# The last group's edge slots and root rows in a relational graph layer: paced over 61 calls in place of 70

## The chip, the cores and the metric

The kernel runs on one core of a Trainium2 chip. The core has five engines with a queue of instructions each: TensorE (PE in the profile, its weight loads PEld), VectorE (DVE), ScalarE (ACT), GpSimd (POOL) and SyncE (SP). The engines run side by side and wait for one another by semaphores; an engine works off its own queue in order. Transfers between device memory and the on-chip memory are issued from the queues of SP, ACT and POOL and share 16 DMA engines. TensorE writes its sums to PSUM, eight banks of 128 x 512 float32.

The metric is device time in microseconds of one execution, as the median of the runs shown. Line numbers (L356) are those of the kernel before.

## The reference

One layer of a relational graph network with a highway gate, over 1250 nodes of 1024 features, 20000 edges and 8 edge types, all in float32:

```python
h = jnp.maximum(_layernorm(x, axis=-1), 0.0)
...
out = h @ root + bias
for r in range(weight.shape[0]):              # 8 types
    mask = (edge_type == r).astype(h.dtype)
    sums = jax.ops.segment_sum(h[src] * mask[:, None], dst, num_segments=n)
    cnt = jax.ops.segment_sum(mask, dst, num_segments=n)
    out = out + (sums / jnp.maximum(cnt, 1.0)[:, None]) @ weight[r]
u = out
z = jnp.concatenate([u, h], axis=1) @ w_gate + b_gate
x = x + jnp.tanh(u) * z + h * (1.0 - z)
```

## The kernel before

**Matrices and pairs.** The order of sums and products is swapped: the kernel multiplies h by each of the eight weights, writes the products y to device memory, and then adds up, for each node, the rows of y that its edges name. Eleven matrices go through TensorE one after the other (the list `mats`): 0 to 7 the weights, 8 the root, 9 the lower half of w_gate (its product with h is the z of the gate, without u's part), 10 the upper half of w_gate, which multiplies u. The 1250 rows are ten blocks `d` of up to 128; blocks i and i + 5 form pair i, 0 to 4. One pair and one matrix are one call of `product`: seven products of 128 x 512 x 512 (a 2 x 2 scheme with seven in place of eight multiplications; some of the seven are split once more in the same way, by `Second` and `Third`, for pairs 0 to 3). The sums of weight blocks that this scheme needs (t1 to t4, L169 to L181) are made by VectorE during pair 4 of the matrix before (t1 to t3) and pair 0 (t4). A product leaves PSUM by a copy on ScalarE (L380, L395, L402, L406, L429) or an addition on VectorE (L373, L381, L389, L309 to L311) into one of four `row` tiles, and a finished row tile is stored by SP (L475): to y for matrices 0 to 7, to `hr_dram` for the root, to `z_dram` for matrix 9. A row tile is filled anew only once its store has landed.

**Calls.** After each of the seven products `done()` calls `between(j)`, j = 0 to 6. So a matrix has 35 calls, and from the start of matrix 8 to the end of matrix 9 there are 70: call 1 is (matrix 8, pair 0, j = 0), call 70 is (matrix 9, pair 4, j = 6). All other work is written into the program at these calls. The schedule is by hand: the order of the program is the order in each engine's queue.

**Edge slots.** Edge types 0 to 4 are group 0, types 5 to 7 are group 1, the last. For each group the nodes are sorted by how many edges they have, so that block d needs only K[g][d] slots; for group 1 these are 20, 10, 8, 7, 7, 6, 5, 5, 4, 3, in sum 75. A slot (`add_slot`) is one gather on POOL of up to 128 rows of y into a tile `got` (L1165) and one multiply-add on VectorE, u = got * w + u (L1170). There are four `got` tiles (GOT), so a gather waits until the multiply-add four slots earlier is through. For group 1 the tile u starts with the sums of group 0, gathered from `u_dram` (L586).

**The generator `edges`.** It yields once a tick, t = -1, 0, 1 and so on. With LATE = 4 the slots stand at t = 4 to 78, block after block, for the last group in the order 4 to 9, then 0 to 3. GOT = 4 ticks after a block's last slot its `to` is called. For blocks 4 to 9 this stores u to `last_dram` (L1373, on SP). For blocks 0 to 3, which stay on the chip as `us`, it is `add_hr`: a gather of the root's rows from `hr_dram` into a `got` tile (L586), and three ticks later the addition to u (L1380). The generator yields 87 times; the first, without work for the engines, is taken before the pacing starts.

**The pacing.** `spread` hands out ticks over calls: with `total` ticks and `parts` calls, at call n it brings the ticks run to `total * n / parts`, rounded up, and at call `parts` runs whatever is left. For the last group `total` is 75 + 2 + 4 = 81 and `parts` is 70.

**The gate.** Matrix 10 needs u transposed. `gate_u(i, j)` prepares pair i of the gate (blocks 2i and 2i + 1) one pair ahead: at j = 2 it gathers rows of h into two `got` tiles and takes tanh(u) on ScalarE (L1445), at j = 3 it transposes u on TensorE (L322) and makes the left sums (L327, L338), at j = 4 it subtracts the h rows (L1453), which frees the two `got` tiles. For gate pair 0 this happens beside pair 4 of matrix 9, the last pair of that matrix, for gate pair 1 beside pair 0 of matrix 10. `gate_load(i + 2, j)` fetches the u of the pair after next back from `last_dram` (L1460) and its root rows by `add_hr`. `gate_rows` gathers x + h and z for the output.

The part of the main function that the change touches, without what it calls:

```python
        blocks = [*range(HELD, ND), *range(HELD)]
        last = edges(LG, blocks, lambda d, u: (add_hr if d < HELD else to_last)(d, u), LATE)
        next(last)
        between = spread(last, sum(K[LG]) + 2 + LATE, 7 * ((NM - 2 - s) * NP + NP - i))
        while s < NM - 1:
            def beside_h(j):
                between(j)
                if (s, i, j) == (NM - 2, NP - 1, 0):
                    gate_bias(0)
                if (s, i) == (NM - 2, NP - 1):
                    gate_u(0, j)

            step(s, i, beside_h)
            s, i = next(steps, (NM, 0))
```

Of the kernel before, what the change touches and what calls it, by code (L numbers as in the profile page):

```python
# [19 lines left out]
def tile_rgcn_highway(  # L20
# [44 lines left out]
    NP = ND // 2  # L65
# [4 lines left out]
    K = ((28, 14, 13, 12, 11, 10, 9, 8, 7, 6), (20, 10, 8, 7, 7, 6, 5, 5, 4, 3))  # L70
# [9 lines left out]
    GOT = 4  # L80
    UB = 4
    LATE = 4
    IDLE = 12

    A11, A12, A22, S1, S2, S3, S4 = range(7)
    A21 = S3
# [34 lines left out]
    def bank():  # L121
        return psum.tile([P, 512], F32, name="ps", bufs=6)
# [318 lines left out]
    NM = len(mats)  # L441
# [125 lines left out]

    for _ in range(IDLE):
        nc.tensor.matmul(bank()[:, :P], ident, ident, start=True, stop=True)
# [72 lines left out]
    with ExitStack() as early:  # L642
# [20 lines left out]
        class Normed:  # L663
# [13 lines left out]
            def spread(self):  # L677
                n = self.n
                nc.vector.bn_aggr(self.mv[:n], self.st[:n].rearrange("p a b -> p (a b)"))
                nc.scalar.activation(self.sd[:n], self.mv[:n, 1:2], AF.Sqrt, bias=eps[:n])  # L680
# [446 lines left out]
        while going[0]:  # L1127
            s, i = next(steps)
# [11 lines left out]
    with ExitStack() as edges_part:  # L1140
# [47 lines left out]
        def edges(g, blocks, to, late=0):  # L1188

            nb = len(blocks)
            starts = [late + sum(K[g][d] for d in blocks[:b]) for b in range(nb + 1)]
            leaves = [starts[b + 1] - 1 + GOT for b in range(nb)]
            reads = [max(-1, starts[b] - 5, leaves[b - UB] if b >= UB else -1) for b in range(nb)]
            u, then = {}, {}
            for t in range(-1, leaves[-1] + 4):
                for b, d in enumerate(blocks):
                    if starts[b] <= t < starts[b + 1]:  # L1200
                        k = t - starts[b]
                        add_slot(u[d], g, d, k, idx[:, g], w_of[:, g])
                for b, d in enumerate(blocks):
                    if t == leaves[b]:
                        then[t + 3] = to(d, u[d])
                if then.get(t):
                    then[t]()
                for b, d in enumerate(blocks):
                    if t == reads[b]:
                        u[d] = first_u(g, d)  # L1210
                yield
# [8 lines left out]
        def spread(e, total, parts):  # L1220

            said = [0, 0]

            def between(j):
                said[0] += 1
                while said[1] < min(total, -(-total * said[0] // parts)):
                    next(e, None)
                    said[1] += 1
                if said[0] == parts:
                    for _ in e:  # L1230
                        pass

            return between
# [27 lines left out]
        def beside(e, total, s, i, last):  # L1261


            between = spread(e, total, 7 * ((last - s) * NP + NP - i))
            while s <= last:
                step(s, i, between)
                s, i = next(steps, (NM, 0))
            return s, i

        s, i = next(steps)  # L1270
        while s <= EARLY:
            step(s, i)
            s, i = next(steps)
# [17 lines left out]
        while s < R0[1]:  # L1291
            step(s, i, on)
            s, i = next(steps)
# [9 lines left out]
        s, i = beside(first_group, sum(K[0]) + LATE + 1, s, i, R0[2] - 1)  # L1303
# [64 lines left out]
        LG = G - 1  # L1368
# [97 lines left out]
        blocks = [*range(HELD, ND), *range(HELD)]  # L1466
        last = edges(LG, blocks, lambda d, u: (add_hr if d < HELD else to_last)(d, u), LATE)
        next(last)
        between = spread(last, sum(K[LG]) + 2 + LATE, 7 * ((NM - 2 - s) * NP + NP - i))
        while s < NM - 1:  # L1470
            def beside_h(j):
                between(j)
# [6 lines left out]
            s, i = next(steps, (NM, 0))  # L1479

        for i in range(NP):
            t = [rows.tile([P, D], F32, name="row") for _ in range(2)]

            def finish(part, of, c0, more=None):
                d = 2 * i + part
                n = nrows(d)
                at = slice(c0, c0 + of.shape[-1])
                to = t[part][:n, at]
                if more is None:
                    nc.vector.tensor_mul(to, of[:n], place_of("d", i, part)[:n, at])  # L1490
                    nc.vector.tensor_add(to, to, place_of("z", i, part)[:n, at])
                else:
                    nc.vector.tensor_mul(more[:n], of[:n], place_of("d", i, part)[:n, at])
                    nc.vector.tensor_add(to, to, more[:n])
# [38 lines left out]
            if i < NP - 1:  # L1533
                product(h_op[i % 2], fac[NM - 1], t, between=beside_u,
                        last=lambda *of: finish(1, *of))
# [28 lines left out]
```

## Time and profile before

| | |
|---|---|
| median of 3 runs | 1376.04 us (1373.76 to 1376.51) |
| the profiled execution | 1373.07 us, its span 1371.1 us |
| TensorE busy | 1344.4 us, 98% of the span |
| VectorE busy | 944.2 us, 69% |
| ScalarE busy | 370.4 us, 27% |
| GpSimd busy | 587.3 us, 43% |
| mean granted TensorE clock | 0.993 |
| multiply-adds of slots, L1170 | 193, 1282 ns each |
| gathers of slots, L1165 | 193, 1298 ns each on POOL |
| device memory read and written | 212.71 MB and 75.66 MB |

A profile is one execution, taken by the hardware profiler. An engine's line gives its busy time; for TensorE, ends are modelled, so busy is not the same as at its peak. A group of instructions is a line of the kernel with engine, operation and tiles, "out<-in", the number of them, busy time and the mean of one, and then the idle time of the engine just before them and who ended it. In the timeline each row is a start, a duration, the engine, the line and the tiles; in brackets stands the idle time before it and its releaser. SPq, ACTq and POOLq are issues of transfers from those queues. The clock is a share of full speed, as the throttle granted it.

### The profile page before, as it was taken

The page shows a single profiled execution, that of the slowest core. Times are in us where ns is not written, and L with a number is a line of the kernel's source. Part 1 is how long each engine was busy: PE and PEld are TensorE (multiplying, and loading weights), DVE is VectorE, ACT ScalarE, POOL GpSimd, SP SyncE. Part 2 cuts the span into 40 slices and gives each one's busy share as a digit, 9 for nine tenths or more (in the row PEclk, how much of TensorE's full clock was granted, in tenths as well). Part 3 has the DMA queues.
Part 4 walks back from the last instruction along what each step waited for, and adds up shares of the span by engine and source line. Part 5 has one row for each costly group of instructions (what it writes and reads, how often), then busy time and mean ns, then how long its engine had stood idle before and what let it go on. Part 6 is the DMA issues. An engine that isn't in the chain of part 4 may idle for free.

```text
span 1371.1 us, 13215 instructions
## 1 busy us (share of the span) xinstructions
PE 1344.4 (98%) x3954; PEld 686.5 (50%) x3954; DVE 944.2 (69%) x1932; ACT 370.4 (27%) x816; POOL 587.3 (43%) x510
## 2 busy tenths in 40 slices
PE   9999999999999999999999999999999999986997
PEld 5444455455445545554554554555455455543443
DVE  6855967876795743426767776877776796656875
ACT  3335566565731111111111111111112111120210
POOL 0001655654562475002444554455356364435641
PEclk9999999999999999999999999999999999998999
DMA  8755766854954351135549689878678936859971
GB/s 306 275 180 149 92 140 142 213 78 116 194 138 109 71 146 22 61 138 184 191 129 329 218 265 354 271 272 294 209 241 317 360 101 219 308 200 280 328 212 58
DMA packets 106908, 271.15 MB, mean 198 GB/s; under 512 B 22692, under 2 KB 24946, under 8 KB 106704
## 3 DMA queue, kind: packets, MB, share of 16 engines
q1 hardware_dynamic: 46640, 120.01, 29.8%
q0 software_dynamic: 44064, 118.28, 27.4%
q10 hardware_dynamic: 16128, 31.98, 7.4%
q8 instruction: 31, 0.51, 0.2%
q14 instruction: 45, 0.37, 0.1%
HBM read 212.71 MB, written 75.66 MB: 210 GB/s over the span
## 4 chain that ended last, share of the span: by engine, by line
PE 75%; issue 9%; DMA 9%; POOL 4%; DVE 2%; SPq 0%; POOLq 0%; ACT 0%; DVEq 0%; ACTq 0%
PE ps L356 60%; PE ps L214 8%; DMA got<-y,idx 6%; PE ps_n L356 3%; DMA got<-hr_dram,node 2%; PE ps_q L214 2%; POOL got L1165 1%; PE ps_n L214 1%; POOL got L586 1%; DMA w<-in_L_gnn_weight_dram 1%; POOL out_dram L592 1%; PE ps_n L903 1%; PE ps L322 0%; POOL h_op L586 0%; POOL w L586 0%
## 5 line engine op out<-in xcount | busy, mean ns | idle before, releaser
L356 PE MATMUL ps<-w,h_op 128*128 128x512 f32 x2512 | 1110.3, 595 | 13.6 <-DVE row L373 11.3
L356 PEld LDWEIGHTS ps<-w,h_op 128*128 128x128 f32 x2512 | 472.7, 191 | 558.2 <-issue 528.4
L1165 POOL DMA_INDIRECT got<-y,idx x193 | 250.6, 1298 | 357.8 <-DVE u L1170 230.8
L1170 DVE SCALAR_TENSOR_TENSOR u<-got,w_of,u 128x1024 f32<-128x1024 f32 (+1 forms) x193 | 247.0, 1282 | 85.5 <-DMA got<-y,idx 82.6
L982 POOL DMA_INDIRECT table<-row_col,at_i x157 | 176.6, 1125 | 157.7 <-DVE at_i L978 73.9
L381 DVE TENSOR_TENSOR row<-row,part 128x512 f32<-128x512 f32 x55 | 37.9, 689 | 123.8 <-ACT part L380 123.8
L429 ACT COPY row<-ps 128x512 f32<-128x512 f32 x50 | 29.3, 585 | 215.5 <-PE ps L356 215.5
L380 ACT COPY part<-ps 128x512 f32<-128x512 f32 x55 | 32.2, 586 | 179.7 <-PE ps L356 179.7
L395 ACT COPY row<-ps 128x512 f32<-128x512 f32 x55 | 32.2, 585 | 175.4 <-PE ps L356 170.7
L214 PE MATMUL ps<-w,w 128*128 128x256 f32 x288 | 71.3, 380 | 0.0
L406 ACT COPY row<-ps 128x512 f32<-128x512 f32 x55 | 32.2, 586 | 139.3 <-PE ps L356 139.3
L214 PEld LDWEIGHTS ps<-w,w 128*128 128x128 f32 x288 | 54.4, 190 | 18.3 <-issue 12.4
L968 DVE SCALAR_TENSOR_TENSOR junk<-k_bc,key_col,before 128x128 f32<-128x128 int32 x157 | 54.9, 350 | 4.2
L908 DVE TENSOR_TENSOR seen<-seen,ps_n 128x100 f32<-128x100 f32 x157 | 40.3, 256 | 24.6 <-PE ps_n L903 20.4
L402 ACT COPY row<-ps 128x512 f32<-128x512 f32 x43 | 25.2, 586 | 115.7 <-PE ps L356 112.1
L214 PE MATMUL ps<-w,h_op 128*128 128x256 f32 x216 | 56.0, 382 | 0.0
L214 PEld LDWEIGHTS ps<-w,h_op 128*128 128x128 f32 x216 | 40.5, 190 | 25.6 <-issue 22.3
L169 DVE TENSOR_TENSOR w<-w,w 128x2048 f32<-128x2048 f32 (+1 forms) x12 | 25.4, 2116 | 39.3 <-PE ps L356 38.2
L885 ACT ACTIVATE is_lo<-io,less_lo 128x128 bf16<-128x128 f32 x157 | 50.2, 391 | 0.7 <-DMA xh_dram<-xt 0.7
L373 DVE TENSOR_TENSOR row<-row,ps 128x512 f32<-128x512 f32 x30 | 20.5, 684 | 37.5 <-PE ps L356 31.3
L623 POOL DMA_INDIRECT node_dram<-ids,pos_i x20 | 28.5, 1426 | 41.1 <-issue 41.1
L356 PE MATMUL ps_n<-w,h_op 128*128 128x512 f32 x96 | 43.2, 592 | 0.0
(215 smaller groups left out, 1183.1 us busy)
## 6 DMA issues: line engine op xcount, KB each, us to landing
y<-row SPq DMA_DIRECT2D x72, 512.0 KB
w<-in_L_gnn_weight_dram ACTq DMA_DIRECT2D x21, 1024.0 KB
w<-in_L_gnn_weight_dram SPq DMA_DIRECT2D x10, 1024.0 KB
k_bc<-keys_dram SPq DMA_DIRECT2D x39, 256.0 KB
l_bc<-los_dram SPq DMA_DIRECT2D x39, 256.0 KB
w<-in_L_gnn_w_gate_dram ACTq DMA_DIRECT2D x6, 1024.0 KB
h_dram<-h_op SPq DMA_DIRECT2D x9, 512.0 KB
u<-in_L_gnn_bias_dram SPq DMA_DIRECT2D x9, 512.0 KB
```

The costliest lines, as they stand in the source:

```text
L214: nc.tensor.matmul(p, a[:, k, :], b[:, k, :], start=(fresh and k == 0), stop=(k == 1), skip_group_check=True)
L356: nc.tensor.matmul(b[:, at], aop[:, i, k, :], w.of[i][:, k, at], start=(fresh and k == 0), stop=(k == KQ - 1), skip_group_check=True)
L380: nc.scalar.copy(d, b)
L381: nc.vector.tensor_add(c22, c22, d)
L395: nc.scalar.copy(c11, b)
L406: nc.scalar.copy(c12, b)
L885: nc.scalar.activation(is_lo[:, i, :], io, AF.Abs, bias=less_lo[:, c0 + i:c0 + i + 1])
L908: nc.vector.tensor_add(seen[j][:, i, :], was, p[:, i, :])
L968: nc.vector.scalar_tensor_tensor(junk, o["k_bc"][:, i, :], key_col[:, c:c + 1], before, op0=OP.is_equal, op1=OP.mult, accum_out=rank[:, c: ...
L982: ins = nc.gpsimd.indirect_dma_start(out=table[:, :], out_offset=bass.IndirectOffsetOnAxis(ap=at_i[:n, i:i + 1], axis=0), in_=row_col[:n, ...
L1165: nc.gpsimd.indirect_dma_start(out=t[:n], out_offset=None, in_=y[g][:, :], in_offset=bass.IndirectOffsetOnAxis(ap=at[:n, d, k:k + 1], axis=0),
L1170: nc.vector.scalar_tensor_tensor(u[:n], t[:n], w, u[:n], op0=OP.mult, op1=OP.add)
```

## The change

A constant AHEAD = 9 is new. The last group's ticks are handed out over nine calls fewer, 61 in place of 70, and `total` is 4 + 75 + 4 + 4 = 87 in place of 81, which is every tick that the generator has. With that the last tick falls on call 61, (matrix 9, pair 3, j = 4). Since calls go on after the last one that is paced, `spread` tests for `>=` in place of `==`. The pacing of the first group, by the same function, is untouched.

```diff
@@ -81,6 +81,7 @@
     UB = 4
     LATE = 4
     IDLE = 12
+    AHEAD = 9
@@ -1226,7 +1227,7 @@
                 while said[1] < min(total, -(-total * said[0] // parts)):
                     next(e, None)
                     said[1] += 1
-                if said[0] == parts:
+                if said[0] >= parts:
                     for _ in e:
                         pass
@@ -1466,7 +1467,8 @@
         last = edges(LG, blocks, lambda d, u: (add_hr if d < HELD else to_last)(d, u), LATE)
         next(last)
-        between = spread(last, sum(K[LG]) + 2 + LATE, 7 * ((NM - 2 - s) * NP + NP - i))
+        between = spread(last, LATE + sum(K[LG]) + GOT + 4,
+                         7 * ((NM - 2 - s) * NP + NP - i) - AHEAD)
         while s < NM - 1:
             def beside_h(j):
                 between(j)
```

## The prediction

> **What bounds the kernel now.** I read the page first (busy shares and slices), then the stages as a table, then who TensorE waits for, then the timeline of the last 170 us engine by engine.
>
> The page's summary and slices (40 slices of 34.3 us):
>
> ```profile
> span 1371.1 us, 13215 instructions
> PE   9999999999999999999999999999999999986997
> PEclk9999999999999999999999999999999999998999
> ```
>
> TensorE sets the end; it has two soft places, slices 36 and 37 and the last. The same by stage; the columns are PE, weight load, DVE, ACT and POOL busy with counts, granted clock, DMA share, GB/s. The stages are matrix 8, matrix 9 up to its last pair, that pair up to the transposes for pair 2 of matrix 10, and one free pair:
>
> ```profile
> 978.39:1095.58 117.19, 117.19 (x330) 61.98 (x329) 82.37 (x103) 19.14 (x37) 57.47 (x47) 1.00 0.82 288
> 1095.58:1188.73 93.15, 93.15 (x273) 51.34 (x272) 71.47 (x90) 16.19 (x32) 47.91 (x37) 1.00 0.60 197
> 1188.73:1274.72 85.99, 71.06 (x177) 32.32 (x176) 56.38 (x58) 16.97 (x24) 40.38 (x30) 0.92 0.79 258
> 1274.72:1300.50 25.78, 25.78 (x73) 12.30 (x72) 22.52 (x27) 5.45 (x8) 15.64 (x14) 1.00 1.01 322
> ```
>
> TensorE is never idle in matrices 8 and 9 until the last pair; only the third stage loses time and clock. TensorE's waits there:
>
> ```profile
> PE ps L356 <- DVE row L373: 11.3, 2, 8.8
> PE ps L322 <- DVE u L1380: 2.7, 1, 2.7
> PE ps L356 <- DVE h_op L327: 0.9, 1, 0.9
> ```
>
> VectorE in turn stands behind slots. Timeline (start, duration, engine, line, operands, idle before and its releaser):
>
> ```profile
> 1199.40 2.75 POOL L586 DMA_INDIRECT got<-h_dram,node  x1 [3.12 <-DVE u L1170]
> 1208.38 1.28 DVE L1170 SCALAR_TENSOR_TENSOR u<-got,w_of,u 128x1024 f32<-128x1024 f32 x1 [4.20 <-DMA got<-y,idx]
> 1209.94 0.99 POOL L1165 DMA_INDIRECT got<-y,idx  x1 [4.53 <-DVE u L1170]
> 1216.41 1.28 DVE L1170 SCALAR_TENSOR_TENSOR u<-got,w_of,u 128x1024 f32<-128x1024 f32 x1 [6.14 <-DMA got<-y,idx]
> 1217.96 0.99 POOL L1165 DMA_INDIRECT got<-y,idx  x1 [7.03 <-DVE u L1170]
> 1246.60 1.23 DVE L1380 TENSOR_TENSOR u<-u,got 128x1024 f32<-128x1024 f32 x1 [8.51 <-DMA got<-hr_dram,node]
> ```
>
> The two h rows for the gate hold two of the four `got` buffers from 1199 until their subtraction at 1226.79, so the last slots go one at a time: gather, 6.5 us, multiply-add, next gather. That pushes the hr gathers of the first gate pair to 1234, into the z stores and u loads, where one takes 12.3 us (1234.32 to 1246.60).
>
> **The change, part by part.** No instruction is added or dropped; ticks move to earlier calls. Before, 81 ticks go over 70 calls (1.157 each) and call 70 runs the rest; after, 87 ticks (the whole generator) go over 61 (1.426 each). Call 61 is pair 3 of matrix 9, j = 4. The `>=` costs nothing: calls 62 to 70 find the generator empty.
>
> *What it takes away.* Call 63 had reached tick 73, so calls 64 to 70 (the last pair) carried slots of t = 73 to 78, six multiply-adds with their gathers, two hr gathers and two hr adds. All go before that pair. What TensorE gets back: the last pair starts at 1188.73 (40 matmuls from 1185.30, the first product of 3.43 us belonging to pair 3), and its transposes come four products later, at 1202.47. Free pairs follow each other every 25.78 us (transposes at 1274.72, 1300.50, 1326.29). So the transposes for pair 2 would stand at 1202.47 + 2 x 25.78 = 1254.03; they stood at 1274.72. **Gain 20.7 us**: 14.9 us of the waits above, 4.7 us of slow clock (8 matmuls in 5.10 us and the next 48 in 23.92, where 3.60 and 20.7 are normal; granted clock 0.50 in 1251 to 1257), 1.1 us of small gaps. From below: if the 8.8 us wait for L373 and its slow clock stay, 20.7 - 8.8 - 4.7 = 7.2.
>
> *What still has to be ready there.* h rows: POOL is free, gathers about 1185, used about 1208. hr rows of gate pair 0 take the h rows' buffers, about 1210, and are added about 1225; 12.3 us, the worst seen, still fits. The u load follows the z stores on SP at about 1216; the slots' lag of 6.5 us gives 1223. VectorE in such a pair is 22.5 of 25.8 us busy without TensorE waiting (last row of the table). I take 1 us lost, between 0 and 3 (the L1380 wait of 2.7).
>
> *What it moves into matrix 8 and 9.* By the end of matrix 8 (call 35) the old pacing had reached tick 41, 37 slots; the new one tick 50, 46 slots. The nine cost VectorE 9 x 1.28 = 11.5 us. VectorE in matrix 8:
>
> ```profile
> L1170 DVE SCALAR_TENSOR_TENSOR u<-got,w_of,u 128x1024 f32<-128x1024 f32 (+1 forms) x36 | 46.0, 1282 | 21.8 <-DMA got<-y,idx 20.9 <-issue 0.7
> L381 DVE TENSOR_TENSOR row<-row,part 128x512 f32<-128x512 f32 x5 | 3.4, 688 | 9.7 <-ACT part L380 9.7
> ```
>
> Busy 82.4 of 117.2, 20.9 waiting for gathers, 11.8 for TensorE (9.7 at L381, 2.1 at L169). So 11.5 fits only into those 11.8, if gather waits do not grow; and they are fixed by the ring: a gather reaches its multiply-add 5.5 to 11.4 us after issue (1052.84 to 1063.02, say), with four buffers. Slot 1 ran at 994.66, slot 37 at 1098.39: 103.7 us for 36 steps, 2.88 each. Of that VectorE waited 11.7 for TensorE; filled with slots, the pitch is (103.7 - 11.7) / 36 = 2.56. The new pacing asks for 117.2 / 50 = 2.35 (50 ticks in 35 calls). Slot 46 at 2.56 comes at 994.66 + 45 x 2.56 = 1109.9, where 1098.4 is on time: **11.4 us late**.
>
> What waits behind a late slot:
>
> ```profile
> 1070.72 0.68 DVE L309 TENSOR_TENSOR row<-row,ps_n 128x512 f32<-128x512 f32 x1
> 1071.42 2.33 SPq L475 DMA_DIRECT2D hr_dram<-row  x3
> 1078.61 0.59 ACT L402 COPY row<-ps 128x512 f32<-128x512 f32 x1 [2.80 <-PE ps L356]
> 1094.88 2.28 DVE L177 TENSOR_TENSOR w<-w,w 128x2048 f32<-128x2048 f32 x1
> 1099.60 2.28 DVE L181 TENSOR_TENSOR w<-w,w 128x2048 f32<-128x2048 f32 x1
> ```
>
> (a) The weight sums of matrix 9: t3 ends at 1097.1 for a product at 1106.7, t4 at 1101.9 for one at 1111.1: cover 9.2 us, so 11.4 - 9.2 = 2.2 us lost. (b) Rows: L309 of pair 3 finishes a tile that SP stores at 1071.4 and that pair 4 refills at 1078.61 (L402), which TensorE needs for its fourth product at 1081.84. The last_dram stores stand in the same SP queue and wait for the slots too. Lateness there is 11.4 x (1070.7 - 994.7) / 103.7 = 8.4; cover 2.6 us (1079.2 to 1081.84) plus whatever the store had landed early, at most 5: lost 0.8 to 5.8. The two do not add, since a TensorE stopped at (b) is no longer early at (a). **I take 5 us lost.** Bounds: at 2.35 nothing; if 2.88 cannot be beaten, 45 x 2.88 makes slot 46 25.9 late, 16.7 lost by (a), about the same by (b). The lag is paid once: matrix 9 loads no weights until its fourth pair (DMA share 0.60 by the second stage row), its gathers need 3.3 to 6 us (1112.63 to 1116.14), and the last slots leave at call 61.
>
> The first slot moves from call 5 to call 4. Its gather still leaves at 988.31, behind the u read; only L245 now stands behind it, and no product needs that for 15 us. Nothing.
>
> **Weighed against the Trainium skill.** By the same table pairs 2, 3 and 4 of matrix 8 moved 328, 328 and 369 GB/s in 23.2, 23.3 and 24.0 us, 24.1 MB, the last at a DMA share of 0.98. The page DMA: Bandwidth & Descriptors, Specifications, puts the HBM limit of one core at about 358 GB/s, which speaks against the change: those 24.1 MB with up to seven gathers of 0.52 MB more would need 27.8 MB / 358 GB/s = 77.6 us of their 70.5, an estimate of 7 us given back, 1363 us. The same page's fit (section Anatomy of one DMA) makes a 512 KB gather about 3.2 us, by which the ring would keep pace and nothing be given back, 1355; the trace's 5.5 to 11.4 us say otherwise in matrix 8.
>
> **Sum.** Span 1371.1 - 20.7 + 1 + 5 = 1356.4. The profiled execution took 1373.07, 2.0 around its span, and lies 3.0 under the median 1376.04; with these 4.9 the forecast is 1361.3.
>
> **Rivals.** *Full gain*: gathers in matrix 8 keep the pitch of 2.35, because lags of 6.1 to 6.9 us (its first six slots) allow (6.5 + 1.3 + 0.5) / 4 = 2.1; against it stand lags of 10 to 11 with DMA at 0.96 to 0.98. 1371.1 - 20.7 + 4.9 = 1355.3. *The wait moves to matrix 8 (slower)*: nine more gathers lengthen the lag instead of filling gaps. At 3.0 per slot (lag 10.2) slot 46 is late by 31.3, 22.1 lost by (a), and a TensorE that stands so long gets the slow clock again, 4.7: 1371.1 - 20.7 + 1 + 26.8 + 4.9 = 1383.1. It turns the sign from 2.84 per slot: 24.2 late, 15.0 plus 4.7 lost. For it: 2.88 was the pitch before, with the POOL queue waiting for L1170 before most gathers. Against: 11.7 us of that were VectorE waiting for TensorE, and every stall lightens the DMA. *It does not do it*: the 8.8 us wait comes from the crowd of z stores and u loads, not from the slots; gain 7.2, 1368.8, and 1373.8 with 5 given back. Against: hr gathers then leave 6 us ahead of those stores.
>
> **How the numbers follow.** Forecast (part given back, 1357 to 1368) 0.60; full gain 0.17; wait moved 0.13; does not do it 0.10. 0.2%, 2.75 us, is about what this kernel's measurement tells from no change. Faster: the first two and the half of the last in which nothing is given back, 0.82; within 0.2%: its other half, 0.05; slower 0.13. Range 1354 (full gain, 1 us of noise) to 1376 (16.7 lost by (a) at the old pitch, with part of the slow clock).
>
> **What would show it.** Right: no L1170 and no L1380 on slots after about 1190; the transposes 25.8 apart from there; no clock below 1.00 around 1250; TensorE idle a few us around 1082 or 1102 to 1111, with releaser ACT row L402 or DVE w. Wrong: no idle in matrix 8 (full gain); idle over 15 us and a low clock there (wait moved); a wait for L373 or L1380 over 5 us still in the first gate pairs.

## The result, and the profile after

The changed kernel takes 1371.73 us (median of 20 runs, 1367.18 to 1375.78) where the kernel before takes 1374.82 (20 runs of its own, 1373.47 to 1378.93): ratio 0.9973, 95% interval 0.9963 to 0.9983. It is faster, by 3 to 4 us; the forecast was 14.7 us faster. The profiled execution took 1371.97 us. Line numbers from here on are those of the changed kernel, one higher than before from the new constant on, two behind the last edit (L309 is now L310, L402 L403, L1170 L1171).

The summary and the slices of the kernel after:

```profile
span 1370.0 us, 13221 instructions
PE   9999999999999999999999999999999799999997
PEclk9999999999999999999999999999999999999999
```

The soft slices 36 and 37 are gone, and slice 32 (1062 to 1096 us) is soft in their place. At the four times of the table before (the columns as there; in this execution matrix 8 starts at 982.27, 3.9 us later, and ends at 1110.52, so the rows no longer fall on the stages):

```profile
978.39:1095.58 117.19, 108.67 (x307) 57.84 (x306) 81.55 (x102) 18.42 (x36) 56.86 (x49) 0.98 0.82 280
1095.58:1188.73 93.15, 90.52 (x246) 47.31 (x245) 76.72 (x84) 13.79 (x28) 58.08 (x42) 0.96 0.67 221
1188.73:1274.72 85.99, 85.99 (x247) 42.89 (x246) 57.18 (x67) 20.54 (x31) 27.97 (x23) 1.00 0.78 251
1274.72:1300.50 25.78, 25.78 (x74) 12.34 (x73) 22.53 (x28) 5.37 (x9) 15.33 (x15) 1.00 1.04 341
```

TensorE's lost time has moved from the third row to the first two, which had none before: 8.5 us idle in the first, all in matrix 8, and 2.6 in the second, in matrix 9. The clock is 0.98 and 0.96 there; the slow stretch after the stop in matrix 8 lies partly in the second row. Whom TensorE waits for in this kernel, from matrix 8 on (total, times, longest):

```profile
PE ps L357 <- ACT row L403: 6.6, 1, 6.6
PE ps_n L357 <- DVE row L310: 2.6, 1, 2.6
PE ps_q L215 <- DVE inner L276: 1.9, 1, 1.9
```

And the last pair of matrix nine with the gate pairs behind it, as TensorE's transposes of u in the timeline:

```profile
1222.00 1.91 PE L323 MATMUL ps<-ident,u 128*128 128x128 f32 x16
1247.78 1.91 PE L323 MATMUL ps<-ident,u 128*128 128x128 f32 x16
1273.57 1.91 PE L323 MATMUL ps<-ident,u 128*128 128x128 f32 x16
1299.35 1.91 PE L323 MATMUL ps<-ident,u 128*128 128x128 f32 x16
```

They are 25.78 us apart from the first one on, as in the free pairs of the kernel before: nothing is lost there.

**A ruler for all the kernels.** What happens before matrix 8 differs from one profiled execution to the next by up to 8 us, though the program is the same there in all of them. So each profile is measured from one mark, the start of the second product of matrix 8, its first into `ps_n` (981.82 us in the kernel before, 985.70 after), to the end of its span. Before: 1371.1 - 981.82 = 389.3. After: 1370.0 - 985.70 = 384.3. Without loss it would be 389.3 - 20.7 = 368.6, so the changed kernel gives back 15.7 us. The ruler sees one execution of a kernel, the ratio all of its runs. The two differ by up to 7 us in the table below, so a difference of a few us between two rulers shows nothing by itself.

Where these 15.7 us lie, by TensorE's timeline against a kernel that stops nowhere (run e9 below): 2.14 up to the last product of pair 3 of matrix 8, 8.91 from there to the second product of matrix 9, with pair 4 between (30.90 us there, 39.81 here), 4.60 from that to the first transposes, and nothing behind them (148.0 us to the end in both).

How TensorE came to stop in pair 4 of matrix 8, the timeline of the kernel after, cut to one chain:

```profile
1065.87 1.28 DVE L1171 SCALAR_TENSOR_TENSOR u<-got,w_of,u 128x1024 f32<-128x1024 f32 x1 [5.52 <-DMA got<-y,idx]
...
1071.44 1.13 PE L215 MATMUL ps_q<-inner,inner 128*128 128x256 f32 x4 [1.88 <-DVE inner L276]
...
1083.36 2.61 DVE L1171 SCALAR_TENSOR_TENSOR u<-got,w_of,u 128x1024 f32<-128x1024 f32 x2 [4.01 <-DMA got<-y,idx]
...
1086.21 0.68 DVE L310 TENSOR_TENSOR row<-row,ps_n 128x512 f32<-128x512 f32 x1
...
1086.92 2.70 SPq L476 DMA_DIRECT2D hr_dram<-row  x3
...
1094.03 0.58 ACT L403 COPY row<-ps 128x512 f32<-128x512 f32 x1 [12.20 <-DMA hr_dram<-row]
...
1094.67 19.44 PE L357 MATMUL ps<-w,h_op 128*128 128x512 f32 x40 [6.63 <-ACT row L403]
```

Read it from the bottom. TensorE waits 6.63 us for a copy on ScalarE; ScalarE has waited 12.20 us for a store of the root's rows; the store was issued at 1086.92 and landed after 7.1 us; it was issued so late because L310, an addition that the row tile still lacked, ran at 1086.21; and L310 stood on VectorE behind multiply-adds that waited 5.52 and 4.01 us for their gathers. No product waits for those multiply-adds; they are only ahead of L310 in VectorE's queue. VectorE's groups in the kernel after, in the time of the first row (978.39 to 1095.58):

```profile
L1171 DVE SCALAR_TENSOR_TENSOR u<-got,w_of,u 128x1024 f32<-128x1024 f32 (+1 forms) x39 | 49.8, 1283 | 33.5 <-DMA got<-y,idx 27.5 <-issue 5.8
L382 DVE TENSOR_TENSOR row<-row,part 128x512 f32<-128x512 f32 x4 | 2.7, 684 | 0.0
```

Before, VectorE waited 9.7 us at L382 for ScalarE, and so for TensorE: it was ahead. Now it never does; its waits for gathers have grown from 20.9 to 27.5 us (28.8 in the whole of its matrix 8, 982.27 to 1110.52).

### The profile page after: what moved, and what is told of

It reads as the page before. It is cut to its first block, busy times and chain, and to the rows that moved or that the text cites. A ratio compares the mean times of both kernels' runs of the same rounds, so it can differ in the third digit from the quotient of the medians.

```text
span 1370.0 us, 13221 instructions
## 1 busy us (share of the span) xinstructions
PE 1344.5 (98%) x3954; PEld 687.1 (50%) x3954; DVE 946.0 (69%) x1932; ACT 369.8 (27%) x816; POOL 579.1 (42%) x510
## 3 DMA queue, kind: packets, MB, share of 16 engines
q0 software_dynamic: 44064, 118.28, 27.5%
## 5 line engine op out<-in xcount | busy, mean ns | idle before, releaser
L1171 DVE SCALAR_TENSOR_TENSOR u<-got,w_of,u 128x1024 f32<-128x1024 f32 (+1 forms) x193 | 246.9, 1282 | 89.9 <-DMA got<-y,idx 81.8
L382 DVE TENSOR_TENSOR row<-row,part 128x512 f32<-128x512 f32 x55 | 37.9, 689 | 106.9 <-ACT part L381 100.0
L215 PEld LDWEIGHTS ps<-w,w 128*128 128x128 f32 x288 | 54.4, 190 | 18.3 <-issue 12.4
L909 DVE TENSOR_TENSOR seen<-seen,ps_n 128x100 f32<-128x100 f32 x157 | 40.2, 256 | 28.4 <-PE ps_n L904 13.4
L403 ACT COPY row<-ps 128x512 f32<-128x512 f32 x43 | 25.1, 585 | 125.5 <-PE ps L357 102.5
L374 DVE TENSOR_TENSOR row<-row,ps 128x512 f32<-128x512 f32 x30 | 20.6, 685 | 42.5 <-PE ps L357 31.5
```

What stands on the lines that cost most here:

```text
L215: nc.tensor.matmul(p, a[:, k, :], b[:, k, :], start=(fresh and k == 0), stop=(k == 1), skip_group_check=True)
L382: nc.vector.tensor_add(c22, c22, d)
L909: nc.vector.tensor_add(seen[j][:, i, :], was, p[:, i, :])
L1171: nc.vector.scalar_tensor_tensor(u[:n], t[:n], w, u[:n], op0=OP.mult, op1=OP.add)
```

## The experiments

Each run is set against runs of the kernel before in the same batch, whose medians were 1374.94 us for e1 to e4, 1372.21 for e5 to e8 and 1376.25 for e9 to e12. "By ratio" is (ratio - 1) times that median; "from the mark" is the ruler above, where 389.3 is before, 384.3 after and 368.6 no loss. e1, e5 and e6 leave out part of the sums: they ask a question and are no kernels to use.

| run | edit | median, us | ratio (95%) | by ratio, us | from the mark |
|---|---|---|---|---|---|
| after | | 1371.73 | 0.9973 (0.9963 to 0.9983) | -3.7 | 384.3 |
| e1 | before, six slots left out | 1358.42 | 0.9879 (0.9858 to 0.9900) | -16.6 | 371.0 |
| e2 | dense in matrix 8 only | 1380.95 | 1.0041 (1.0028 to 1.0054) | +5.6 | 397.1 |
| e3 | dense in matrix 9 only | 1374.89 | 0.9998 (0.9986 to 1.0009) | -0.3 | 392.1 |
| e4 | row tile not waited for | 1370.39 | 0.9960 (0.9944 to 0.9975) | -5.5 | 384.1 |
| e5 | half the rows gathered | 1358.75 | 0.9902 (0.9888 to 0.9917) | -13.4 | 371.5 |
| e6 | half the columns added | 1357.04 | 0.9897 (0.9882 to 0.9912) | -14.1 | 368.6 |
| e7 | AHEAD = 5 | 1360.08 | 0.9899 (0.9886 to 0.9912) | -13.9 | 377.5 |
| e8 | paced by hand to call 65 | 1361.17 | 0.9924 (0.9910 to 0.9938) | -10.4 | 382.7 |
| e9 | AHEAD = 0, total 87 | 1356.73 | 0.9878 (0.9849 to 0.9908) | -16.8 | 368.6 |
| e10 | AHEAD = 3 | 1363.94 | 0.9910 (0.9893 to 0.9928) | -12.4 | 378.8 |
| e11 | AHEAD = 7 | 1371.39 | 0.9962 (0.9946 to 0.9978) | -5.2 | 386.6 |
| e12 | AHEAD = 9, total 81 | 1365.62 | 0.9914 (0.9894 to 0.9935) | -11.8 | 376.5 |

**e1: the gain alone.** The kernel before, with one condition more:

```diff
-                    if starts[b] <= t < starts[b + 1]:
+                    if starts[b] <= t < starts[b + 1] and (g < G - 1 or t < 73):
```

> The kernel before, with its old pacing, but without the last group's six slots of t = 73 to 78 (six gathers and six multiply-adds, part of the sums of blocks 2 and 3, are left out of the computation), so that nothing but the root rows runs beside the last pair of matrix nine. It asks for the gain alone: no slot is moved into matrices 8 and 9. Theory 1 (the gain is real and was given back earlier): 15 to 20 us under the kernel before, transposes of the gate pairs about 25.8 us apart, no TensorE wait in matrices 8 and 9; not all 20.7, because the hr gathers still come late. Rival (the late slots were never the cause, the hr gathers beside z stores and u loads were): 3 to 8 us under it, with the 8.8 us wait for the addition into row still there.

Measured: 16.6 us under the kernel before. TensorE's waits from matrix 8 on are down to one:

```profile
PE ps L356 <- DVE row L373: 2.7, 1, 2.7
```

So the six slots beside the h rows were nearly the whole loss, and the rival (z stores and u loads as the cause) falls. The 2.7 us still there follow an addition of root rows (L1380) that waits 1.06 us for its hr gather just ahead of L373.

**e2 and e3: where density costs.** The pacing is replaced by a list of (call, tick) points with straight lines between them:

```diff
-        between = spread(last, LATE + sum(K[LG]) + GOT + 4,
-                         7 * ((NM - 2 - s) * NP + NP - i) - AHEAD)
+        stages = [(0, 0), (35, 50), (63, 73), (70, 81)]      # e2
+        stages = [(0, 0), (35, 41), (61, 87)]                # e3
+        ...
```

> Only the density of matrix 8 is changed: tick 50 by call 35 as in the changed kernel, then slower, so that call 63 stands at tick 73 and call 70 at tick 81 as before the change. It has the price in matrix 8 without the gain. Theory 1 (the row tile's store behind late slots stops TensorE in matrix 8): 9 to 12 us over the kernel before: about 6.6 wait for the copy into row in pair 4 of matrix 8, 1.9 for inner, 2 to 3 of slow clock. Rival (what is given back is given back in matrix 9, the waits in matrix 8 are cover that would come back there): within 3 us of before.

> Matrix 8 at its old pace (tick 41 by call 35), matrix 9 takes all the rest by call 61 (46 ticks in 26 calls, 2.0 us each where the pitch in matrix 8 was 2.56). Theory 1 (lateness comes from gathers against weight loads and hr stores in matrix 8, matrix 9 with half the transfers has room): the whole gain less some us, 12 to 17 under the kernel before. Rival 1b (VectorE's own chain is the limit wherever the slots stand: 16 slots more of 1.28 us fill matrix 9's 21.7 us of free VectorE time): the wait comes back at the addition into row from ps_n in pairs 1 to 3 of matrix 9 and the time is within 5 us of before, 0 to 5 under it.

e2 waits at the same two places of matrix 8 as the changed kernel, and still pays at the last pair (L374):

```profile
PE ps L357 <- DVE row L374: 10.8, 2, 10.5
PE ps L357 <- ACT row L403: 7.1, 1, 7.1
PE ps_q L215 <- DVE inner L276: 2.4, 1, 2.4
PE ps L323 <- DVE u L1381: 1.5, 1, 1.5
```

It is slower by 5.6 us, not 9 to 12 (7.8 from the mark), in part because this time the last pair's stops came to 12.3 us where the kernel before had 14.9; the 9.5 us in matrix 8 are as expected. e3 has no stop in matrix 8, and stops in matrix 9 instead:

```profile
PE ps_n L357 <- DVE row L310: 12.0, 1, 12.0
PE ps_q L215 <- DVE inner L276: 5.7, 2, 4.4
```

By ratio it ends where the kernel before ends. Matrix 9, which moves fewer bytes, did not take slots at 2.0 us: the last 30 followed each other by 2.69 us ((1202.49 - 1124.36) / 29), no faster than in matrix 8. Rival 1b holds, and theory 1 in its first form (transfers of matrix 8 as the cause) falls.

**e4: take the waiting place away.** S4's product of pair 4 gets a PSUM bank and an addition of its own, and the copy into the row tile comes one product later:

```diff
-        nc.scalar.copy(c22, c)
+        if not apart:
+            nc.scalar.copy(c22, c)
...
+            if apart:
+                e = psum.tile([P, 512], F32, name="ps_q", bufs=1)
+                add(e, S4, True)
+                nc.vector.tensor_add(c12, c12, c)
+                nc.vector.tensor_add(c12, c12, e)
```

> The changed kernel, but in pair 4 of matrices 8 and 9 the copy of S1's product into the row tile comes one product later and S4's product goes to a free PSUM bank with one more addition on VectorE (0.7 us), so that TensorE's fourth product doesn't wait for a row tile whose store has not landed. The result is the same. Theory 1a (the row tile's store is the place where lateness reaches TensorE): the 6.6 us wait and its 2.1 of slow clock go, 6 to 9 us under the changed kernel, 9 to 12 under the one before. Rival 1b (VectorE's lateness is the limit and shows at the next wait instead): the stop moves to inner, w or ps_n a few products on; at most 3 us under the changed kernel.

The 6.6 us wait is gone, and the time from the mark is 384.1 against 384.3. TensorE now stops a little later, for VectorE directly:

```profile
PE ps_q L215 <- DVE inner L276: 5.4, 2, 5.1
PE ps_n L357 <- DVE row L310: 2.5, 1, 2.5
PE ps L357 <- DVE w L174: 1.0, 1, 1.0
PE ps L357 <- DVE row L246: 0.9, 1, 0.9
PE ps L357 <- DVE w L178: 0.8, 1, 0.8
PE ps L357 <- DVE w L182: 0.2, 1, 0.2
```

By ratio it is 1.8 us better than the changed kernel, and the intervals overlap. A wait taken away at one place comes back at the next, because it is VectorE's queue that is late, not that row tile: every one of the new waits is for VectorE.

**e5 and e6: gathers or additions?** Both halve one side of each slot of the last group:

```diff
-            n = nrows(d)
+            n = nrows(d) if g < G - 1 else nrows(d) // 2                      # e5
...
-            nc.vector.scalar_tensor_tensor(u[:n], t[:n], w, u[:n], ...)
+            c = slice(0, D if g < G - 1 else D // 2)
+            nc.vector.scalar_tensor_tensor(u[:n, c], t[:n, c], w, u[:n, c], ...)   # e6
```

> The changed kernel, but the last group's slots gather and add only the first half of each block's rows (64 partitions of 128; the sums of the other nodes lack these edges). VectorE's multiply-add has as many columns as before, so VectorE's busy time stays; the gathers' bytes halve. Theory L (the ring's lag is what makes VectorE late: gather waits of 27.5 us in matrix 8 and 15.9 in matrix 9): lags fall, slots keep the pitch of 2.35, no wait in matrices 8 and 9, 14 to 18 us under the kernel before. Theory V (VectorE's busy time is what makes it late): within 3 us of the changed kernel, 0 to 6 under the one before, with the same waits.

> The changed kernel, but the last group's multiply-adds take only the first 512 of 1024 columns (the other half of these sums is left out); gathers are as they were. A multiply-add should fall from 1.28 to about 0.65 us, 47 us of VectorE's time over 75 slots. Theory V: no wait in matrices 8 and 9, 15 to 18 us under the kernel before. Theory L: the ring's pitch falls only by the multiply-add's share of its round, 0.63 / 4 = 0.16, to 2.40 where 2.35 is wanted; slot 46 is then about 2 us late instead of 9 to 11, so that most of the waits go too: 11 to 15 under it, with gather waits of VectorE longer than 27.5 us in matrix 8.

Either one brings most of the gain back: 371.5 and 368.6 from the mark, 13.4 and 14.1 us by ratio. In e5, where a multiply-add takes as long as ever, only one stop is left:

```profile
1084.00 19.13 PE L357 MATMUL ps<-w,h_op 128*128 128x512 f32 x40 [1.99 <-ACT row L403]
```

In e6 there is none (its profiled execution, 1352.44 us, is the fastest of four; the slowest took 1360.56), though VectorE waits for gathers longer than in any other kernel (its group in matrix 8):

```profile
L1172 DVE SCALAR_TENSOR_TENSOR u<-got,w_of,u 128x512 f32<-128x512 f32 (+2 forms) x45 | 34.1, 762 | 42.9 <-DMA got<-y,idx 37.0 <-issue 5.4
```

A multiply-add of half the columns takes 750 ns in matrix 9, where all have that form (0.65 us was expected; the 762 here are a mean over other forms too). So theory V falls: in e5 VectorE's multiply-adds take as long as before, and all stops but one are gone. Theory L, which counts the multiply-add as part of a slot's round on the ring of four, has e6's time and its longer gather waits; e5 came out at 13.4 us (interval 11.4 to 15.4) where it had 14 to 18. But L made e6's pitch 2.40, and it is less: the first 46 slots followed each other by 2.56 us in the changed kernel ((1114.10 - 998.85) / 45), by 2.38 in e5 and 2.27 in e6, where 2.35 is asked; all 75 by 2.64, 2.45 and 2.34. So the ring's round alone doesn't set the pitch. The rest of VectorE's work stands in the same queue; shorten the gathers or the multiply-adds, and the pace is met or nearly so.

**e7 and e8: less density.**

```diff
-    AHEAD = 9
+    AHEAD = 5                                              # e7
...
+        stages = [(0, 0), (7, 9), (14, 19), (21, 28), (28, 37), (35, 45),
+                  (42, 52), (49, 62), (56, 72), (63, 83), (65, 87)]     # e8
+        ...
```

> The changed kernel with AHEAD = 5: 87 ticks over 65 calls, the last just ahead of the gathers of h rows at call 66. A slot is wanted every 2.50 us (117.2 / 46.8) in place of 2.35. If lateness is what costs (pitch 2.56 at best): slot 43 is at most 3 us late, under the cover of the row tile; no wait in matrix 8, 12 to 16 us under the kernel before. If slots or root rows that close to the last pair bring back its waits: within 4 us of the kernel before, with the wait for the addition into row from ps or for u there.

> As with AHEAD = 5, but the ticks are handed out by hand: 9 and 10 to a pair where VectorE was idle for 6 us or more (matrix 8 pairs 1 to 3, matrix 9 pairs 1 to 3) and 7 to 8 where it makes weight sums (pair 4 of matrix 8, pair 0 of matrix 9, in which it is busy 22.9 of 23.2 us). If VectorE's lateness at the weight sums and rows is the cause, the time is 1 to 4 us under that of the even pace over 65 calls, 14 to 17 under the kernel before. If the denser stretches bring waits of their own (inner, ps_n), it is over it, 8 to 12 under the kernel before.

Four calls more are worth 10 us. e7's forecast was met in time, but not in full: it still stops 4.65 us for L310 and 1.97 for `inner` in matrix 9. The hand-made pacing e8 is no better than the even one (10.4 against 13.9 us by ratio, the intervals just overlapping). The time is its rival's, but the rival's reason, denser stretches, does not explain the first of its two stops: at no call of matrix 8 has e8 asked for more ticks in all than e7. Still TensorE stops for L403 in pair 4 of matrix 8 (4.90 us) and in the last pair of matrix 9 (4.65):

```profile
1087.00 19.88 PE L357 MATMUL ps<-w,h_op 128*128 128x512 f32 x40 [4.90 <-ACT row L403]
1211.55 5.31 PE L357 MATMUL ps<-w,h_op 128*128 128x512 f32 x8 [4.65 <-ACT row L403]
```

Ahead of the L310 of the first stop VectorE has the same 31 slots in both kernels. The idle time before them differs, and L310 runs 3.2 us later by the mark in e8 (e7 above, from 983 to 1072.6 us, e8 below, from 983 to 1075.8):

```profile
L1171 DVE SCALAR_TENSOR_TENSOR u<-got,w_of,u 128x1024 f32<-128x1024 f32 (+1 forms) x31 | 39.6, 1283 | 22.4 <-DMA got<-y,idx 14.2 <-issue 7.8
L1171 DVE SCALAR_TENSOR_TENSOR u<-got,w_of,u 128x1024 f32<-128x1024 f32 (+1 forms) x31 | 39.7, 1283 | 27.4 <-DMA got<-y,idx 25.9 <-issue 1.2
```

This execution of e8 took 1366.68 us, where four of its six runs took 1360.13 to 1361.31, so the two stops need not be in all of them.

**e9 to e12: the two halves of the change, and the steps between.** The change has two edits, `total` from 81 to 87 and nine calls fewer. Each alone is e9 and e12:

```diff
-    AHEAD = 9
+    AHEAD = 0                                              # e9 (3: e10, 7: e11)
...
-        between = spread(last, LATE + sum(K[LG]) + GOT + 4,
+        between = spread(last, sum(K[LG]) + 2 + LATE,      # e12
```

> One half of the change alone: AHEAD = 0, so 87 ticks go over all 70 calls (81 before). The last slot, tick 78, falls on call 63 in place of call 68, ahead of the two h rows that hold got tiles from call 66; only the last block's root rows run beside the last pair. A slot is wanted every 2.69 us, over the pitch of 2.56 that matrix 8 reached, so no lateness. Theory 1 (six slots beside the h rows were the whole loss, the pitch of 2.56 the whole price): no wait in matrices 8 and 9, one of up to 3 us in the first gate pairs, 14 to 18 us under the kernel before, as without the six slots. Rival (the root rows' gathers at calls 66 to 69 behind the h rows bring the waits back): 5 to 10 under it.

> The other half of the change alone: AHEAD = 9 with total = 81 as before, so that call 61 runs ticks 82 to 87 (no slot among them) at once. A slot is wanted every 2.52 us, nearly as with AHEAD = 5, and the last slot falls on call 59 as there. Theory 1 (what counts is the pitch and that no slot stands beside the h rows): the same as AHEAD = 5 within 2 us, 12 to 16 under the kernel before. Rival (the two are late for another reason, the place of the last tick): the same as the changed kernel, 2 to 5 under the one before.

> AHEAD = 3: 87 ticks over 67 calls, a slot every 2.58 us, just at the pitch of 2.56. Theory 1: no wait over 2 us in matrix 8, the same or up to 3 us under AHEAD = 5, 14 to 18 under the kernel before. Rival (the waits of 4.65 for ps_n and 1.97 for inner in matrix 9 with AHEAD = 5 are not lateness of slots but collisions of single instructions): the same time as AHEAD = 5 within 1.5 us, with waits of 2 to 5 us somewhere in matrix 9.

> AHEAD = 7: 87 ticks over 63 calls, a slot every 2.43 us in place of 2.35 and 2.50. Theory 1: slot 45 is 45 x (2.56 - 2.43) = 6 us late, half of that past the cover; 3 to 7 us of waits with slow clock, between AHEAD = 9 and AHEAD = 5: 6 to 11 us under the kernel before. Rival (a threshold between 5 and 9 that is met or not): 3 or 14 under it.

e9 has the lowest ratio of the kernels that do the whole computation, 0.9878, though its interval overlaps e7's. Its profiled execution, 1355.11 us, has no loss in any stage:

```profile
978.39:1095.58 117.19, 117.19 (x329) 61.98 (x328) 83.36 (x104) 19.15 (x37) 58.59 (x48) 1.00 0.82 288
1095.58:1188.73 93.15, 93.15 (x273) 51.34 (x272) 76.97 (x92) 16.21 (x32) 55.25 (x40) 1.00 0.64 215
1188.73:1274.72 85.99, 85.99 (x237) 40.74 (x236) 68.13 (x77) 19.46 (x28) 43.45 (x34) 1.00 0.92 300
```

and the chain that stops the changed kernel holds, ScalarE's 3.38 us of waiting being covered (two of its six runs took 1363.83 and 1366.70 us; no trace shows what those lost, or where):

```profile
1073.39 0.68 DVE L310 TENSOR_TENSOR row<-row,ps_n 128x512 f32<-128x512 f32 x1
...
1081.86 0.59 ACT L403 COPY row<-ps 128x512 f32<-128x512 f32 x1 [3.38 <-DMA hr_dram<-row]
```

e12 came out 2 us over e7 by ratio and 1 under it from the mark, near to what theory 1 had, if just outside its 12 to 16; its stop (4.74 us for L403) is in matrix 8, where e7's are in matrix 9. e11 lies between 5 and 9, a little worse than expected. e10 is the miss: 2.58 us a slot should have been as free as e9 and is not better than e7, as the rival had it. It stops 2.21 us for L310 in pair 2 of matrix 9 and 4.55 for L403 in the last pair; there a slot and a root row (L1381 at 1195.38) ran just ahead of L310 at 1196.85. So the even pace alone doesn't decide. By the timelines, which slot falls ahead of which row, and how long its gather takes, can move a stop by some microseconds; no run changed these alone.

**One row tile, nine kernels.** The chain in pair 4 of matrix 8 can be added up. TensorE needs the refilled bank 100.02 us after the mark (1081.84 - 981.82 in the kernel before). It gets it when L310, plus the time until ScalarE starts (with the store's issue and landing), plus the copy's 0.59 us, are through:

| kernel | L310 after the mark | L310 to the copy's start | copy's end past 100.02 | stop measured |
|---|---|---|---|---|
| before | 88.90 | 7.89 | under 0 | none |
| e9 (2.69 us a slot) | 88.91 | 8.47 | under 0 | none |
| e10 (2.58) | 89.73 | 7.06 | under 0 | none |
| e7 (2.50) | 90.73 | 7.57 | under 0 | none |
| e11 (2.43) | 93.11 | 9.71 | 3.39 | 3.28 |
| e5 (2.35) | 93.44 | 8.10 | 2.11 | 1.99 |
| e8 (by hand) | 93.91 | 10.54 | 5.02 | 4.90 |
| e12 (2.52) | 94.31 | 9.98 | 4.86 | 4.74 |
| after (2.35) | 100.51 | 7.82 | 8.90, less the 2.14 lost earlier: 6.76 | 6.63 |

The sum gives each stop to within 0.13 us. All its terms are measured in the same execution, so it is bookkeeping: it shows that this chain, and nothing else, stops TensorE there. In the first row and in e10 ScalarE waited for TensorE at that point, so their second column is an upper bound; elsewhere it waited for the store, 7.6 to 10.5 us. So L310 may be late by 100.02 - 0.59 - 88.90 = 10.5 less that: 0 to 3 us and no more. What makes it late is not the number of slots alone: e7, e8 and e12 have 31 ahead of it, and VectorE's idle time before them was 22.4, 27.4 and 27.6 us. That difference of 5 us is larger than the free time.

**What the density bought.** The last slot's multiply-add started 214.5 us after the mark in e9 (1198.94 - 984.48), and 208.2 us in the changed kernel (1193.88 - 985.70): the program asks for it eight calls earlier (call 55 in place of 63), some 27 us at 117.19 / 35 = 3.35 us a call, and it comes 6 us earlier. Asked for 2.35 to 2.58 us, the evenly paced kernels with whole slots (after, e7, e10 to e12) got 2.64 to 2.70 over all 75. What is asked beyond that becomes lateness of what stands behind a slot in VectorE's queue.

## Why the prediction went wrong, step by step

- **The gain of 20.7 us: right in the traces.** 389.3 - 368.6 from the mark is 20.7, in e9 and in e6; over all their runs they are 16.8 us (12.7 to 20.8) and 14.1 (12.1 to 16.2) under the kernel before. In the changed kernel the transposes are 25.78 us apart with the clock at 1.00, and neither L374 nor L1381 is waited for.
- **1 us lost in the gate pairs: nothing was lost.** 148.0 us from the first transposes to the end, with and without AHEAD.
- **The pitch of 2.56 us: met, by luck as far as the runs show.** It was 2.56 over the first 46 slots, and the waits for TensorE that were to be filled (11.8) were filled. But gather waits, which were not to grow, went from 20.9 to 27.5 us, TensorE itself stood still for 8.5 us in that time, and e7, e10, e11 and e12, asked for 2.43 to 2.58, got 2.69 to 2.75 over the same slots. Longer gather waits are no loss by themselves: e9 has 26.7 us of them in its matrix 8 (981.05 to 1098.24).
- **(b), the row tile, 0.8 to 5.8 us: the place and the chain were right, the size wrong**: 8.91 us. Three terms: L310 was 11.6 us late (100.51 - 88.90), 9.5 without TensorE's own earlier stop, where 8.4 was worked out by scaling slot 46; the cushion "whatever the store had landed early, at most 5" was 0.1 us, for the copy could start only 7.82 us after L310, which leaves 10.53 - 7.82 = 2.7 of cover where the sum had 2.6 without the cushion; and the stretch lost 2.28 us besides the stop of 6.63, with the slow clock after it, a price that the sum had put only on its slow rival.
- **(a), the weight sums, 2.2 us lost: not reached.** A TensorE that has stopped at (b) is no longer early there, as the prediction said; only in e4, where (b) is gone, do the weight sums stop it (1.0, 0.8 and 0.2 us).
- **A stop that no step had**: 1.88 us for L276 ahead of (b), for the same late queue; up to (b) it cost 2.14.
- **"The lag is paid once": this is the step that failed by its reason.** Matrix 9 paid again, 4.60 us:

```profile
1162.67 0.68 DVE L310 TENSOR_TENSOR row<-row,ps_n 128x512 f32<-128x512 f32 x1
1163.40 5.40 PE L357 MATMUL ps_n<-w,h_op 128*128 128x512 f32 x8 [2.63 <-DVE row L310]
```

  The argument was that matrix 9 loads no weights until its fourth pair and gathers are quick there. But quick gathers are not free VectorE time: e3, asked for 2.0 us a slot there, got 2.69. The pacing asks for 2.35 us a slot until call 61, the kernel manages 2.64 over all 75, so the lateness is made anew all the way; e7 stops in matrix 9 without any stop in matrix 8. Added up, where the sum gave back 5 + 1 = 6 us, the trace gave back 2.14 + 8.91 in matrix 8 and 4.60 in matrix 9.
- **The weighing against the Trainium skill.** The page DMA: Bandwidth & Descriptors, Specifications, with about 358 GB/s of HBM for a core, gave an estimate of 7 us given back. The bytes that it took for granted did not come: e6, with the same gathers of 128 rows and no stop, moved 346, 361 and 259 GB/s in its pairs 2 to 4 (23.3, 23.3 and 24.0 us), which is 22.7 MB and not 27.8. So e6 does not try the estimate. The limit was not a ceiling, for the kernel before moved 369 GB/s over the 24.0 us of pair 4. Another page, Perfetto Trace Analysis, section Roofline, says that 358 is a core's share when both cores of a pair use the memory and that a single active core can pull more, up to some 120% of it. This kernel runs on one core, and the measured 369 agrees with that page: the prediction took the line that doesn't fit a core alone.
- **The rivals.** The wait did move to matrix 8, as the slower rival had it; its price, 26.8, was too high because it took a pitch of 3.0. What no case considered is that the change has two halves that can be had apart: `total` = 87 alone (e9) asks for the last slot at call 63, ahead of the last pair.

## What to carry to other kernels

Background work that is written into the queue of an engine off the critical path has a rate that its own buffers and that engine allow; measure the rate (here 2.6 to 2.7 us a slot), and ask for no more than that: 2.69 was free in its trace (e9), 2.58 was not (e10). Asked for more, the work comes little earlier (6 us for 27): it delays whatever urgent instruction stands behind it, at one place after another, so that taking one wait away is worth little (e4, at most 1.8 us by ratio and nothing from the mark). More `got` buffers, or another place for L310 in the queue, were not tried. And cost a late instruction along its whole chain, to the landing of the store it feeds: the free time behind L310 was 10.5 us, and the store took 7.6 to 10.5 of it. One profile is one execution; where stops hang on a few microseconds, as here, set it beside the times of all runs.

## What was not expected of the hardware

- A stop of TensorE often costs more than itself: eight products that take 3.60 us took 5.40 after a stop of 2.63, 5.39 after 4.65 (e7), 5.16 after 2.53 (e4) and 6.61 after 4.55 (e10). The granted clock was 0.66 in the 6 us around the end of the 6.63 us stop and 0.77 in the next 6. But eight took 3.70 after 2.21 (e10), and 48 took 20.87, where 20.7 is normal, after 2.66 (e1). The Trainium skill (TensorE: Matmul & The Clock Gate, Why this matters for your kernels) advises against gaps of TensorE over about 3 us. The runs are stricter: 2.63 us had its price. That 2.66 us in e1 had none fits what the page says of the gate in What's actually happening, that its window runs free of the kernel, so that equal stops can fall differently in it; no run here shows the window itself.
- Half the columns are not half the time on VectorE: a multiply-add took 750 ns at 512 columns (e6) and 1283 at 1024. If the time is a straight line in the columns, an estimate from these two is 2 x 750 - 1283 = 217 ns that do not depend on them.
